# Two graph layers in fp32: layer-norm scale and shift folded into the next weights, pairwise masks, and one value bias moved behind the output weights

## The chip, the cores and the metric

One core of one Trainium2 chip runs the whole kernel. The metric is the device time of the program in microseconds; the kernel before takes 3042.13 us, the median of three runs between 3041.22 and 3043.72 us. All arithmetic is in fp32.

## The reference

The input is `x`, 64 graphs of 256 nodes with 256 features, and `adj`, a 0/1 matrix of 256 by 256 for each graph. Two layers follow each other.

```python
# layer 0
h = gat(gat(x, adj, W1, a1), adj, W2, a2)            # softmax over leaky_relu(e) where adj > 0
h = layernorm(x + h) * g_ln1 + b_ln1
x = layernorm(h + relu(h @ w_ff1 + b_ff1) @ w_ff2 + b_ff2) * g_ln2 + b_ln2
# layer 1: 8 heads of 32; r is the relation, the value of adj
attn = softmax((x @ Wq + bq) @ (x @ Wk + bk).T / sqrt(32))
out = sum over r of (attn * (adj == r)) @ (x @ Wv[r] + bv[r])
x = layernorm(x + out @ Wo + bo) * g1 + beta1
x = layernorm(x + gelu(x @ W1 + b1) @ W2 + b2) * g2 + beta2
```

Four layer norms end the four stages: after the two graph attentions, after the first feed-forward, after the relational attention, and after the second feed-forward. Since `adj` is 0 or 1, only two relations occur; the kernel uses `Wv[0]` for all weights and the difference `Wv[1] - Wv[0]` for the masked ones.

## The kernel before

The 64 graphs are worked in 32 pairs. `whole_way(pair)` takes one pair through everything: `gat_layers`, `feed_forward` with relu, `attention`, `feed_forward` with gelu. Each of these is a generator that yields before each group of matmuls and names what the group waits for. Up to four pairs are on their way at a time, so that TensorE has groups of several pairs to choose from.

The order of the work is planned while the program is built. `put(engine, us, emit, *events, rank=...)` hands a piece of work for an engine other than TensorE to a planner, with the time that the piece is expected to take and the events it waits for; `took(us)` does the same for a group of matmuls. `run` steps through this planned time, takes from each engine's pieces the ready one of lowest rank, and for TensorE prefers groups that have been ready for `SLACK` = 0.3 us. `keep_order` then fixes the instruction order of every engine as planned. Each engine works its queue in that order: an instruction that waits holds up all behind it. Buffers have planned release times too (`needs`, `frees`). So other expected times or other pieces change the order on every engine.

The parts that the change touches:

- `layernorm` (L572): DVE computes mean and variance of the rows in two halves (L582, L583) and two small operations, variance plus eps (L584) and the negated mean (L585). GpSimd raises to the power -0.5 (L588) and multiplies (L589); this short part on GpSimd is called the root below. ACT normalises the rows in place (L593). DVE multiplies by g and adds beta, two operations of 128x512 (L598). The rows so scaled are both the input of the next stage and its residual.
- `transposed` (L607): the rows are turned on DVE in 32x32 blocks (L618), stored to DRAM and gathered (L623, L629), which gives them transposed for the next matmuls. In five cases, named in `hurried`, TensorE transposes instead (`transposed_on_tensor`, L649 and L653). `add_rows` (L570) later adds the residual to a matmul's result.
- `feed_forward`: the first matmuls (L681) follow a scheme with seven products per block instead of eight, with copies by ACT (L687), additions by DVE (L392) and activations by ACT (L693); then the second matmuls (L712).
- `attention`: queries, keys (L754) and values (L759) by the same scheme; queries and keys get their bias from ACT (L769), both value blocks from DVE (L775). `scores` (L796) fills four PSUM banks, one for each of four heads; ACT takes the exponential of each (L803), DVE multiplies each by the mask (L807) and adds its halves (L811). `products` (L825, L828) uses these tiles, and DVE divides (L837, L838). `into_rows` (L847) multiplies by `Wo`.
- `relieve`, `relieve_values` and `reliefs` (from L904): once at the start. Since b2 of a stage is added to beta beforehand (L899), the residual carries it; the biases of the next stage are corrected for it by small matmuls (L912, L921), and sums of weight blocks are made (L340). The queries' weights are scaled (L936).

At the start SP issues the loads of all weights one after the other, and DVE has the additions of L899 and L901 in its queue among the first pairs' work.

Of the kernel before, what the change touches and what calls it, by code (L numbers as in the profile page):

```python
# [18 lines left out]
P = 128  # L19
# [6 lines left out]
EVEN = 1e-37  # L26
HURRIED = 2
# [5 lines left out]
def two_layers(ctx: ExitStack, tc: tile.TileContext, t: dict, out: bass.AP, flag: bass.AP):  # L33
# [77 lines left out]
    a2, w1T = (work.tile([P, 512], F32, name="a", bufs=2 * HQ) for _ in range(2))  # L111
    junk = work.tile([P, N], F32, name="h", bufs=2 * HQ)
    w1T = w1T.rearrange("p (c m) -> p c m", c=KC)
# [28 lines left out]
    free = {name: [0.0] * n for name, n in (("bank", 8), ("a", 2 * HQ), ("m", 2 * HQ), ("h", 2 * HQ), ("yb", 1), ("yT", 2), ("yTa", 1),  # L142
# [372 lines left out]
    def gat_layers(pair, to, loads):  # L515
# [36 lines left out]
        for b in range(2):  # L552
            yield [e[b][1], loads[2]], None, 1
            ps = bank()
            for i in range(2):
                for j in range(2):
                    nc.tensor.matmul(ps[:, i * D:(i + 1) * D], lhsT=e[b][0]["e"][:, j, i * P:(i + 1) * P],  # L557
                                     rhs=z[:, 2 * b + j, :D], start=j == 0, stop=j == 1)
            there = took(1.73)
            frees_at(there.time, ["e"])  # L560
            added = add_rows(to["x"], ps, b, there, loads[2])
            transposed(to["x"], layernorm(to["x"], ln[0], b, added, biased[0]), normal, b, pair, 0)
# [9 lines left out]
    def layernorm(r, gb, b, *events):  # L572
        g, beta, _ = gb
# [3 lines left out]
        def statistics():  # L577
            nonlocal st, mv, rstd, less
            st, mv = small.tile([P, 2, 6], F32, name="st"), small.tile([P, 2, 2], F32, name="mv")
            rstd, less = small.tile([P, 2], F32, name="rstd"), small.tile([P, 2], F32, name="less")  # L580
# [3 lines left out]
            nc.vector.tensor_scalar(rstd, mv[:, :, 1], EPS, None, ALU.add)  # L584
            nc.vector.tensor_scalar(less, mv[:, :, 0], -1.0, None, ALU.mult)  # L585

        def root():
            nc.gpsimd.tensor_tensor(rstd, rstd, mhalf[:, :2], ALU.pow)  # L588
# [6 lines left out]
        def scale():  # L595
            both = r[:, of_graph(b), :]
            for v, op in ((g, ALU.mult), (beta, ALU.add)):
                nc.vector.tensor_tensor(both, both, v.rearrange("p (k d) -> p k d", k=1).to_broadcast([P, 2, D]), op)  # L598

        there = put("vector", 1.22, statistics, *events)  # L600
        there = put("gpsimd", 1.2, root, there)
        return put("vector", 1.2, scale, put("scalar", 0.8, normalise, there))
# [5 lines left out]
    def transposed(y, ready, to, b, pair, stage):  # L608
# [23 lines left out]
        there = put("vector", 0.62, turn, ready, needs="yb")  # L632
        there = put("sync", 0.4, store, there, lag=1.3, kb=256, frees=["yb"])
        to[b] = put("sync", 1.75, gather, there, *([to[0]] if b else []), lag=1.7, kb=64, needs=None if b else "yT")

    def transposed_on_tensor(y, to):

        for b in range(2):
# [17 lines left out]
            to[b] = put("scalar", 0.55, copy, took(0.75), frees=["bank"])  # L656

    def feed_forward(y, normal, w, func, relieved, gb, pair, stage):
# [6 lines left out]
        if hurried(pair, stage):  # L665
            yield from transposed_on_tensor(y, normal)
# [38 lines left out]
        for b in range(2):  # L705
# [12 lines left out]
            normal[b] = layernorm(y, gb, b, add_rows(y, p2, b, there), *([biased[1]] if onwards else []))  # L718
            if onwards:
                transposed(y, normal[b], normal, b, pair, 1)  # L720
        done_with("ff")


    def attention(y, normal, pair, all_adj):


        if hurried(pair, 1):
            yield from transposed_on_tensor(y, normal)
# [13 lines left out]
        a, m, h = ([[None] * HQ for _ in range(4)] for _ in range(3))  # L742
# [29 lines left out]
        def with_bias_v(r, b, event, frees=()):  # L772
            def copy():
                bias = bv[:, r * D:(r + 1) * D].rearrange("p (k d) -> p k d", k=1).to_broadcast([P, 2, D])
# [13 lines left out]
        def scores(n):  # L788
# [10 lines left out]
            adj = all_adj[:, of_graph(b), :].rearrange("p k n -> p (k n)")  # L799

            def weight(o):
                a[n][o] = work.tile([P, 512], F32, name="a", bufs=2 * HQ)
                nc.scalar.activation(a[n][o], ps[o], AF.Exp)  # L803

            def mask(o):
                m[n][o] = work.tile([P, 512], F32, name="m", bufs=2 * HQ)
                nc.vector.tensor_tensor(m[n][o], a[n][o], adj, ALU.mult)  # L807

            def halves(o):
                h[n][o] = work.tile([P, N], F32, name="h", bufs=2 * HQ)  # L810
                nc.vector.tensor_tensor(h[n][o], a[n][o][:, :N], a[n][o][:, N:], ALU.add)  # L811

            there = [put("scalar", 0.48, lambda o=o: weight(o), there, rank=0, function="exp", needs="a", frees=["bank"])
                     for o in range(HQ)]
            masked.append([put("vector", 0.61, lambda o=o: mask(o), there[o], rank=0, needs="m") for o in range(HQ)] +
                          [put("vector", 0.34, lambda o=o: halves(o), there[o], rank=0, needs="h") for o in range(HQ)])

        def products(n):
            b, c = divmod(n, KC)
            po = bank()  # L820
            for r, e in enumerate((a[n], m[n])):
                for jc in range(2):
                    for o in range(HQ):
                        at = r * D + (c * HQ + o) * DH
                        nc.tensor.matmul(po[o * DH:(o + 1) * DH, :N], lhsT=v[:, b, jc, at:at + DH],  # L825
                                         rhs=e[o][:, jc * N:(jc + 1) * N], start=r == jc == 0, stop=r == jc == 1)
            for o in range(HQ):
                nc.tensor.matmul(po[o * DH:(o + 1) * DH, N:], lhsT=ones, rhs=h[n][o], start=True, stop=True)  # L828
            there = took(2.2)
            frees_at(there.time, ["a", "m"] * HQ + ["h"] * (HQ - 1))  # L830
            s, to = h[n][0], qk[:, 0, c, b * N:(b + 1) * N]
# [568 lines left out]
```

## Time and profile before

| | |
|---|---|
| median of the runs | 3042.13 us |
| span of the profiled execution | 3047.2 us (the page gives no other time for it) |
| TensorE matmuls, 19146 records | 2996.3 us busy |
| TensorE weight loads | 2452.5 us |
| VectorE (DVE), 5993 instructions | 2556.8 us |
| ScalarE (ACT), 4096 instructions | 1752.5 us, of it 70 table loads of 1.283 us |
| GpSimd (POOL), 518 instructions | 252.6 us |
| DMA | mean 68 GB/s, 20.6% of 16 engines on the main queue |

Every fp32 matmul instruction leaves two records. The busy time of an engine is the time in which at least one of its instructions is under way; matmuls overlap their neighbours, so a matmul of 128x256 lasts 0.38 us in the records although they start 0.216 us apart when TensorE runs full. The weight loads (PEld) run beside the matmuls. In a line of a group the columns are line, engine, operation, tiles, shapes and count, then the busy time, the mean of one in ns, the idle time of the engine just before, and what ended it. In a line of waits the columns are the engine and tile that waited, for whom, the total in us, how many times, and the longest.

### The profile page before, as it was taken

The numbers are of one execution on the slowest core, as the hardware profiler recorded it, in microseconds if no ns is written. First come the engines' busy times: TensorE is split into PE (matmuls) and PEld (weight loads), VectorE is DVE, ScalarE is ACT, GpSimd is POOL, SyncE is SP. The second block draws the span as 40 slices with busy tenths as digits, with TensorE's granted clock in tenths as the row PEclk, the third lists the DMA queues.
The fourth block names the chain that finished last, engine by engine and source line by source line (L and its number), as shares of the span: only waits on it lengthen the run. The fifth ranks groups of instructions, "written<-read, shape, count | busy, mean of one in ns | idle before, by whom it ended". The sixth has DMA issues, their size and how long they took to land.

```text
span 3047.2 us, 52870 instructions
## 1 busy us (share of the span) xinstructions
PE 2996.3 (98%) x19146; PEld 2452.5 (80%) x19146; DVE 2556.8 (84%) x5993; ACT 1752.5 (58%) x4096; POOL 252.6 (8%) x518
## 2 busy tenths in 40 slices
PE   7999999999999999999999999999999999999998
PEld 6887788878888888888888888888888888788876
DVE  5888988788988888888889888889888898888875
ACT  4556666556556556555565565565555655555654
POOL 0100010001100001100001000011000011000100
PEclk8999999999999999999999999999999999999999
DMA  5211041212212222112222112221122221122100
GB/s 186 74 47 61 32 127 54 70 56 84 70 40 66 77 84 77 53 53 70 84 84 77 39 60 77 84 77 62 50 68 79 84 77 52 52 71 70 49 1 22
DMA packets 211147, 205.76 MB, mean 68 GB/s; under 512 B 22336, under 2 KB 170432, under 8 KB 210880
## 3 DMA queue, kind: packets, MB, share of 16 engines
q1 hardware_dynamic: 210464, 202.06, 20.6%
q8 instruction: 153, 2.51, 0.4%
q14 instruction: 114, 0.93, 0.1%
q10 hardware_dynamic: 416, 0.26, 0.0%
HBM read 137.51 MB, written 64.73 MB: 66 GB/s over the span
## 4 chain that ended last, share of the span: by engine, by line
PE 63%; DVE 25%; DMA 6%; ACT 2%; SPq 1%; issue 1%; POOL 0%; DVEq 0%; ACTq 0%; POOLq 0%
PE ps L712 21%; PE ps L681 15%; PE ps L825 5%; DVE x L598 4%; PE ps L759 4%; PE ps L754 4%; PE ps L544 3%; DVE h L837 3%; PE ps L796 3%; DMA home<-yb 3%; DVE st L582 2%; DVE m L807 2%; PE ps L557 2%; DMA rows<-row 2%; DVE ff L392 2%; PE ps L847 2%
## 5 line engine op out<-in xcount | busy, mean ns | idle before, releaser
L712 PE MATMUL ps<-w_L_gnn_w_ff,ff 128*128 128x256 f32 x2048 | 470.9, 381 | 0.0
L712 PE MATMUL ps<-w_L_gnn_W,ff 128*128 128x256 f32 x2048 | 456.1, 380 | 1.8 <-ACT ff L693 1.8
L593 ACT ACTIVATE x<-x,less,rstd 128x256 f32<-128x256 f32 x512 | 279.2, 596 | 294.8 <-POOL less L589 294.7
L712 PEld LDWEIGHTS ps<-w_L_gnn_w_ff,ff 128*128 128x128 f32 x2048 | 386.6, 190 | 61.5 <-issue 9.8
L712 PEld LDWEIGHTS ps<-w_L_gnn_W,ff 128*128 128x128 f32 x2048 | 388.2, 190 | 57.6 <-ACT ff L693 2.6
L588 POOL TENSOR_TENSOR rstd<-rstd,mhalf 128x2 f32<-128x2 f32 x256 | 198.3, 775 | 2765.7 <-DVE less L585 2638.0
L807 DVE TENSOR_TENSOR m<-a,adj 128x512 f32<-128x512 f32 x512 | 350.1, 684 | 57.9 <-ACT a L803 57.8
L803 ACT ACTIVATE a<-ps 128x512 f32<-128x512 f32 x512 | 268.0, 604 | 222.6 <-PE ps L796 222.5
L681 PE MATMUL ps<-yT,w_L_gnn_W1p 128*128 128x256 f32 x1280 | 315.2, 382 | 4.7 <-ACT ff L687 2.4
L392 DVE TENSOR_TENSOR ff<-ps,ff 128x512 f32<-128x512 f32 x384 | 262.7, 685 | 66.4 <-PE ps L681 58.3
L681 PE MATMUL ps<-yT,w_L_gnn_w_ff1p 128*128 128x256 f32 x1280 | 308.8, 382 | 6.8 <-ACT ff L687 5.9
L681 PEld LDWEIGHTS ps<-yT,w_L_gnn_w_ff1p 128*128 128x128 f32 x1280 | 240.6, 190 | 50.8 <-ACT ff L687 18.8
L687 ACT ACTIVATE ff<-ps 128x512 f32<-128x512 f32 x384 | 223.9, 590 | 98.4 <-PE ps L681 97.6
L681 PEld LDWEIGHTS ps<-yT,w_L_gnn_W1p 128*128 128x128 f32 x1280 | 240.2, 190 | 48.2 <-ACT ps L835 8.5
L837 DVE RECIPROCAL h<-ps 128x256 f32<-128x256 f32 x128 | 223.4, 1746 | 21.3 <-PE ps L828 20.9
L509 ACT ACTIVATE xw<-xw,rs 128x258 f32<-128x258 f32 (+1 forms) x256 | 115.9, 502 | 200.7 <-DVE rs L504 200.6
L693 ACT ACTIVATE ff<-ff,c_L_gnn_b_ff 128x256 f32<-128x256 f32 x384 | 171.6, 504 | 97.4 <-DVE ff L392 97.0
L693 ACT ACTIVATE ff<-ff,c_L_gnn_b 128x256 f32<-128x256 f32 x384 | 173.3, 501 | 85.0 <-DVE ff L392 83.8
L811 DVE TENSOR_TENSOR h<-a 128x256 f32<-128x256 f32 x512 | 213.9, 418 | 0.0
L582 DVE BATCH_NORM_STATS2 st<-x 128x6 f32<-128x256 f32 x512 | 206.0, 402 | 0.9
L570 DVE TENSOR_TENSOR x<-ps,x 128x512 f32<-128x512 f32 x256 | 170.2, 682 | 16.4 <-PE ps L712 9.3
L769 ACT ACTIVATE qk<-ps,bqk 128x256 f32<-128x256 f32 x256 | 106.6, 468 | 112.2 <-PE ps L754 111.9
(128 smaller groups left out, 5008.1 us busy)
## 6 DMA issues: line engine op xcount, KB each, us to landing
home<-yb SPq DMA_DIRECT2D x182, 256.0 KB, 2.0
yT<-home SPq DMA_DIRECT2D x728, 64.0 KB, 2.0
rows<-row SPq DMA_DIRECT2D x60, 512.0 KB, 4.0
input<-in_xT SPq DMA_DIRECT2D x32, 512.0 KB, 5.1
x<-in_x SPq DMA_DIRECT2D x32, 512.0 KB, 3.8
out<-x SPq DMA_DIRECT2D x32, 512.0 KB, 5.1
input<-in_adjT SPq DMA_DIRECT2D x30, 512.0 KB, 4.5
v<-in_adjT SPq DMA_DIRECT2D x2, 512.0 KB, 7.3
```

The source lines that it names most:

```text
L392: nc.vector.tensor_tensor(self.target(c, h), self.bank[bank], self.target(c, h), ALU.add)
L582: nc.vector.bn_stats(st[:, j, :], rows[j])
L588: nc.gpsimd.tensor_tensor(rstd, rstd, mhalf[:, :2], ALU.pow)
L593: nc.scalar.activation(rows[j], rows[j], AF.Identity, bias=less[:, j:j + 1], scale=rstd[:, j:j + 1])
L681: nc.tensor.matmul(to, lhsT=w1[:, a, (t + slab) * P:(t + slab + 1) * P], rhs=b, **flags)
L687: return put("scalar", 0.5, lambda: nc.scalar.activation(target(c, h), blocks.bank["x"], AF.Copy), event, rank=-1)
L693: evacuated[h][m] = put("scalar", 0.4, lambda m=m, to=to, source=source: nc.scalar.activation(to, source, func, bias=b1[:, m:m + 1]), even ...
L712: nc.tensor.matmul(p2[:, j * D:(j + 1) * D], lhsT=f[m][:, (2 * j + b) * P:(2 * j + b + 1) * P], rhs=w2[:, m, :], start=m == 0, stop=m == N ...
L803: nc.scalar.activation(a[n][o], ps[o], AF.Exp)
L807: nc.vector.tensor_tensor(m[n][o], a[n][o], adj, ALU.mult)
L811: nc.vector.tensor_tensor(h[n][o], a[n][o][:, :N], a[n][o][:, N:], ALU.add)
L837: there = put("vector", 1.68, lambda: nc.vector.reciprocal(s, po[:, N:]), there, rank=0)
```

## The change

1. The rows that leave a layer norm toward the next matmuls are no longer scaled and shifted: they are turned as soon as ACT has normalised them. The factor g is multiplied into the next stage's first weights at the start (`with_g`), and beta, by small matmuls, into its biases (`with_beta`, `on_rows`). The residual is scaled and shifted on GpSimd, in place, after the turn has read the rows (`scaled`); `add_rows` waits for that. The last layer norm's rows, which are the output, are scaled on GpSimd too. The two small operations of the statistics go from DVE to GpSimd.
2. Exponentials of two heads share a tile of 128x1024; DVE makes masks and half sums for two heads with one instruction. The buffers hold the same bytes in half as many tiles.
3. The bias of the first value block is no longer added to the values: since the softmax weights of a row sum to one, it is multiplied by `Wo` at the start and added to the row that the residual gets. The values of that block are copied out of PSUM by ACT, without a bias.
4. SP loads three more small columns net, one more bias row and one more bias column, and in part in another order.

The planner's expected times change with the pieces: 0.9 for the statistics, 1.5 for the root, with rank 0, 1.2 for each GpSimd operation with rank 2, 1.14 and 0.61 for the masks and half sums of two heads.

```diff
-        transposed(to["x"], layernorm(to["x"], ln[0], b, added, biased[0]), normal, b, pair, 0)
+        transposed(to["x"], layernorm(to["x"], b, added), normal, b, pair, 0)
...
         def root():
+            nonlocal rstd, less
+            rstd, less = small.tile([P, 2], F32, name="rstd"), small.tile([P, 2], F32, name="less")
+            nc.gpsimd.tensor_scalar(less, mv[:, :, 0], -1.0, None, ALU.mult)
+            nc.gpsimd.tensor_scalar(rstd, mv[:, :, 1], EPS, None, ALU.add)
             nc.gpsimd.tensor_tensor(rstd, rstd, mhalf[:, :2], ALU.pow)
             nc.gpsimd.tensor_tensor(less, less, rstd, ALU.mult)
...
-        def scale():
+        there = put("vector", 0.9, statistics, *events)
+        there = put("gpsimd", 1.5, root, there, rank=0)
+        return put("scalar", 0.8, normalise, there)
+
+    def scaled(r, gb, b, *events):
+
+        def scale(v, op):
             both = r[:, of_graph(b), :]
-            for v, op in ((g, ALU.mult), (beta, ALU.add)):
-                nc.vector.tensor_tensor(both, both, v.rearrange("p (k d) -> p k d", k=1).to_broadcast([P, 2, D]), op)
-
-        there = put("vector", 1.22, statistics, *events)
-        there = put("gpsimd", 1.2, root, there)
-        return put("vector", 1.2, scale, put("scalar", 0.8, normalise, there))
+            nc.gpsimd.tensor_tensor(both, both, v.rearrange("p (k d) -> p k d", k=1).to_broadcast([P, 2, D]), op)
+
+        there = put("gpsimd", 1.2, lambda: scale(gb[0], ALU.mult), *events, rank=2)
+        return put("gpsimd", 1.2, lambda: scale(gb[1], ALU.add), there, gb[2], rank=2)
...
         there = put("vector", 0.62, turn, ready, needs="yb")
+        to["scaled", b] = scaled(y, ln[stage], b, there)
...
-            normal[b] = layernorm(y, gb, b, add_rows(y, p2, b, there), *([biased[1]] if onwards else []))
+            normal[b] = layernorm(y, b, add_rows(y, p2, b, there, normal["scaled", b]))
             if onwards:
                 transposed(y, normal[b], normal, b, pair, 1)
+            else:
+                normal[b] = scaled(y, ln[3], b, normal[b])
...
         def with_bias_v(r, b, event, frees=()):
+            if r == 0:
+                return put("scalar", 0.5, lambda: nc.scalar.activation(target_v(r, b), of_v.bank["x"], AF.Copy), event, rank=-1)
+
...
-            def mask(o):
-                m[n][o] = work.tile([P, 512], F32, name="m", bufs=2 * HQ)
-                nc.vector.tensor_tensor(m[n][o], a[n][o], adj, ALU.mult)
-
-            def halves(o):
-                h[n][o] = work.tile([P, N], F32, name="h", bufs=2 * HQ)
-                nc.vector.tensor_tensor(h[n][o], a[n][o][:, :N], a[n][o][:, N:], ALU.add)
...
+            def weight(q):
+                a[n][q] = work.tile([P, 2, 512], F32, name="a", bufs=HQ)
+                for k in range(2):
+                    nc.scalar.activation(a[n][q][:, k], ps[2 * q + k], AF.Exp)
+
+            def mask(q):
+                m[n][q] = work.tile([P, 2, 512], F32, name="m", bufs=HQ)
+                nc.vector.tensor_tensor(m[n][q], a[n][q], adj, ALU.mult)
+
+            def halves(q):
+                h[n][q] = work.tile([P, 2, N], F32, name="h", bufs=HQ)
+                nc.vector.tensor_tensor(h[n][q], a[n][q][:, :, :N], a[n][q][:, :, N:], ALU.add)
...
-    bv = on_all("L1_gnn_bv", 2 * D)
+    bv, bv0 = on_all("L1_gnn_bv1", D), column("L1_gnn_bv0")
+    less_bv = work.tile([P, 2, 512], F32, name="ff", bufs=NF // 2)[:, 0, :D]
+    nc.sync.dma_start(less_bv, bass.AP(tensor=t["L1_gnn_bv"].tensor, offset=t["L1_gnn_bv"].offset, ap=[[0, P], [1, D]]))
...
+    def with_g(blocks, g, there, more=1.0):
+
+        def scale():
+            for _, c, at in BLOCKS:
+                nc.vector.tensor_scalar(blocks(at), blocks(at), g[:, c:c + 1], more, ALU.mult, ALU.mult)
+
+        return put("vector", 1.4, scale, *there, rank=5)
...
+        g, beta = ln[1][3]
+        q, k = (slice(n * P, (n + 1) * P) for n in range(2))
+        there = [with_beta(bqk[:, n], block(wqk, rows), P, beta) for n, rows in enumerate((q, k))]
+        values = [on_rows(bv, beta, lambda c: block(wv)(1, c)), with_beta(bv0, block(wv), D, beta)]
+        scaled_bias = put("vector", 0.15, lambda: nc.vector.tensor_scalar(bqk[:, 0], bqk[:, 0], SCALE, None, ALU.mult), there[0])
+        there = [with_g(lambda at, rows=rows: wqk[:, at, rows], g, there[n:n + 1], (SCALE, 1.0)[n]) for n, rows in enumerate((q, k))]
+        put("vector", 0.0, lambda: None, block_sums(wqk, put("vector", 0.0, lambda: None, *there)), scaled_bias,
+            block_sums(wv, with_g(lambda at: wv[:, at], g, values)), event=relieved[1])
+        yield values, None, 1
+        on_rows(ln[1][1], bv0, lambda c: wo[:, c], projected, event=ln[1][2])
```

## The prediction

> **What bounds the kernel now.** I read the engine table first, then the stretches, then what TensorE (PE) waited for in the steady part, then the groups on the engines that the change touches.
>
> ```profile
> span 3047.2 us, 52870 instructions
> ...
> PE 2996.3 (98%) x19146; PEld 2452.5 (80%) x19146; DVE 2556.8 (84%) x5993; ACT 1752.5 (58%) x4096; POOL 252.6 (8%) x518
> ```
>
> PE is busy for all but 50.9 us of the span. VectorE (DVE) at 84% is next; GpSimd (POOL) is nearly free. The stretches (columns: length, then busy time and instructions of PE, PEld, DVE, ACT, POOL, then clock and DMA) tell where the 50.9 us lie:
>
> ```profile
> 0.00:30.00 30.00, 18.06 (x88) 15.45 (x89) 12.89 (x40) 9.51 (x21) 0.70 (x6) 0.89 0.80 252
> 30.00:62.00 32.00, 22.75 (x119) 19.75 (x118) 19.07 (x64) 12.71 (x34) 2.34 (x4) 0.79 0.58 180
> ...
> 100.00:2900.00 2800.00, 2786.37 (x17629) 2282.06 (x17631) 2397.14 (x5595) 1628.58 (x3807) 236.67 (x482) 1.00 0.21 67
> 2900.00:2980.00 80.00, 77.91 (x679) 59.92 (x672) 64.22 (x128) 47.83 (x111) 4.74 (x10) 1.00 0.01 1
> 2980.00:3012.00 32.00, 29.50 (x246) 22.80 (x244) 23.37 (x59) 15.46 (x34) 4.25 (x8) 1.00 0.05 17
> 3012.00:3036.00 24.00, 23.70 (x110) 20.49 (x110) 9.08 (x19) 10.56 (x23) 0.88 (x2) 1.00 0.07 23
> 3036.00:3047.00 11.00, 0.00 (x0) 0.00 (x0) 3.14 (x11) 1.09 (x2) 0.88 (x2) 0.63 0.18 54
> ```
>
> 21.2 us are lost in the first 62, only 13.6 in the 2800 us between 100 and 2900, 4.9 from there to 3036, and 11 behind the last matmul. What PE waited for in the middle:
>
> ```profile
> PE ps L681 <- ACT ff L687: 7.4, 15, 1.4
> PE ps L754 <- ACT qk L769: 1.3, 3, 0.8
> PE ps L544 <- ACT xw L509: 1.0, 1, 1.0
> PE ps L825 <- DVE m L807: 1.0, 3, 0.3
> ```
>
> It waits for ScalarE (ACT), hardly for DVE. So the kernel is bound by PE's own work, and DVE's 84% is cover, not path. The groups to be changed:
>
> ```profile
> L593 ACT ACTIVATE x<-x,less,rstd 128x256 f32<-128x256 f32 x512 | 279.2, 596 | 294.8 <-POOL less L589 294.7
> ...
> L588 POOL TENSOR_TENSOR rstd<-rstd,mhalf 128x2 f32<-128x2 f32 x256 | 198.3, 775 | 2765.7 <-DVE less L585 2638.0
> L807 DVE TENSOR_TENSOR m<-a,adj 128x512 f32<-128x512 f32 x512 | 350.1, 684 | 57.9 <-ACT a L803 57.8
> ```
>
> ACT already stands 294.7 us behind POOL's small root; ACT is what PE waits for. That is the thread to watch.
>
> [...]
>
> ```profile
> 51.38 0.70 POOL L588 TENSOR_TENSOR rstd<-rstd,mhalf 128x2 f32<-128x2 f32 x1 [50.07 <-DVE less L585]
> ...
> 57.46 1.20 POOL L588 TENSOR_TENSOR rstd<-rstd,mhalf 128x2 f32<-128x2 f32 x1 [5.06 <-DVE less L585]
> ```
>
> The second ran beside L598 on DVE (two SBUF inputs), the first beside an add from PSUM. That DVE is held by POOL no run here shows[...].
>
> **The change, part by part.** *DVE.* Gone are the 512 scale and shift operations of L598 (88.6+88.6+86.6+86.4 = 350.2 us) and the two small operations L584 and L585 (43.5+41.4 = 84.9). [...] Half of L775 goes to ACT: -43.9. In all -552.8. New at the start are 20 multiplications of weights by g against 4 of L936: between 0.22 us (a 128x128 at L936) and 0.69 (a 128x512 two-input), some 7 us. DVE ends near 2011 us, 66%. Of this PE gets nothing directly: its waits for DVE in the middle are the 1.0 us above and 0.6 for a yT. What it can get is a calmer ACT, since ACT waits for DVE before L693 and L509; the ceiling is the 13.6 us.
>
> *ACT.* 64 copies of values out of PSUM at the 590 ns of L687, which has that shape, are 37.8 us. In the compiled order ACT loads its tables 96 times instead of 70 in this part of the program; at the 1283 ns of the trace's loads, 33.4 us more. ACT ends near 1824 us, 60%; it has room, but each load stands ahead of whatever is queued behind it, 1.3 us at a time.
>
> *POOL.* [...] The roots get two small operations each, about the 209 ns of L589: 256 x 0.42 = 107. [...] The scaled rows are wanted only by the residual addition (L570 before) at the end of the next stage, some tens of us later, so the new wait there costs nothing in the steady part. What is queued behind a scale operation is the next root. [...] the two small operations add 0.4 and take 0.25 off DVE. On the other hand the two L598, 1.38 us, are off the way from a layer norm to its transposition. So the rows come about 1 us earlier, and the ACT instruction (L593) about 0.3 us later.
>
> *DVE held by POOL.* [...] With 34% of DVE free I take no cost for it on PE and keep 0 to 15 us for the range.
>
> *PE.* Four tiny matmuls more; the changes of kind (128 groups of scores, 128 of products) are the same number. Matmuls that wait for two semaphores or more rise from 329 to 443. In the trace of before 507 such extra waits stand in PE's queue, and 94 of them beside a start that is 0.1 us late: 114 x 94/507 x 0.1 = 2 us; 0 to 11.
>
> *Start.* SP issues three more DMAs ahead of the row that DVE's L899 waits for (beta before, b2 now): at 0.47 us each, 1.4 us. Behind that instruction on DVE stand the weights of the attention, behind them ACT's L509, and for that PE stood 9.3 us at L557. So +1.4 on the path; five DMAs in all stand ahead of the third pair's loads, which only ACT's copy of the adjacency meets (high end 3). The multiplications by g fall in DVE's 3.2 and 3.4 us waits before L446 and cost nothing there.
>
> *End.* [...] In the last pair's transpositions by PE, 1.4 us of L598 leave a way on which PE idled 2.5 us between 2980 and 3012: -1.5 (0 to -2.5).
>
> *Sum:* start +1.4, PE's waits +2, end -0.4, middle 0 (from -10 to +15): +3. The profiled execution took its span, 3047.2 us, for which the page gives no other time; that is 5.1 us above the median of the runs, 3042.1. I work the difference in the span and put it on the median: 3045.
>
> **Rivals.** *The middle fills.* With rows 1 us earlier and a freer DVE, ten of the 13.6 us vanish and the extra semaphores hide: 3042.1 + 1.4 - 0.4 - 10 = 3033. For it: 1.4 us less on every layer norm. Against: PE's waits end on ACT's L687, which the change doesn't shorten.
>
> *Late roots.* A root that is behind a scale piece keeps ACT at its L593; behind it stand L687 and L693, and behind these PE. This is the case on the other side: 256 roots, each costing PE 0.06 us on average, are 15 us: 3042.1 + 1 + 15 = 3058. It decides from about 0.02 us per root (6 us). For it: 294.7 us of ACT already wait there, 102 times in the middle with up to 9.2 us[...]. Against: PE has four pairs to choose from and lost only 13.6 us despite those waits.
>
> *Table loads.* A third of the 33.4 us on ACT reaching PE, with the 1 us of start and end: 3054.
>
> **How the numbers follow.** Forecast (PE full as before, 3036 to 3050) 0.40; the middle fills (3026 to 3037) 0.28; late roots (3047 to 3075) 0.26; table loads (3047 to 3062) 0.06. About 6 us, 0.2%, is what the runs can tell from no change. Faster: 0.26 from the second case and 0.02 from the first, 0.28. Slower: 0.25 and 0.06 from the last two and 0.07 from the first, 0.38. The rest, 0.34, is the same. The range 3028 to 3064 leaves out some 0.1 at each end.
>
> **What would show it.** Right: DVE near 2010 us, ACT near 1824 with 26 table loads more, [...]PE still 98%, idle 10 to 17 us between 100 and 2900, and 1 to 3 us more before the first L557. Late roots: ACT's wait for POOL above 400 us and PE's for L687 grown. Wrong: a POOL piece over 2 us, masks much over 1.3 us (DVE held by POOL), or PE's busy share below 97%.

## The result: 36 us slower, outside the range

The changed kernel takes 3078.78 us (3077.64 to 3079.83, four runs), the kernel before, in runs beside it, 3042.93 us (the ratio is 1.0117, 95% interval 1.0103 to 1.0132). 3045 had been forecast, with a range up to 3064. ACT's sum came much as forecast; DVE's sum and TensorE's idle time didn't. Top of the page of the changed kernel:

```profile
span 3075.9 us, 52423 instructions
...
PE 3010.9 (98%) x19154; PEld 2454.7 (80%) x19154; DVE 2234.0 (73%) x4411; ACT 1835.1 (60%) x4186; POOL 1032.2 (34%) x1542
```

DVE lost 323 us of work, ACT gained 83, POOL 780. PE still reads 98%: at that rounding the share can't show 28.7 us of a longer span. (The spans differ by 28.7 us and the medians by 36: other spans here are about 2 us under the time of their run, as 3075.9 is under 3077.64 in the changed kernel, so the 3047.2 of the trace before stands for a run of some 3049, 7 above the median, and losses read from that trace may be too high by so much in all.) The stretches can (columns as before):

```profile
0.00:30.00 30.00, 20.84 (x87) 17.78 (x88) 13.00 (x42) 9.45 (x21) 0.69 (x6) 0.89 0.80 249
30.00:62.00 32.00, 20.81 (x126) 17.49 (x125) 18.73 (x62) 12.53 (x35) 5.20 (x9) 0.79 0.67 183
100.00:2900.00 2800.00, 2768.66 (x17463) 2257.53 (x17462) 2073.75 (x4063) 1697.26 (x3863) 963.09 (x1438) 1.00 0.21 67
```

The first 62 us lose 20.4 us (21.2 before). The middle loses 31.3 us against 13.6: the place is the steady part. What PE waited for there:

```profile
PE ps L689 <- ACT ff L695: 22.9, 29, 1.7
PE ps L545 <- ACT xw L510: 2.6, 1, 2.6
PE ps L689 <- ACT ps L850: 1.8, 1, 1.8
```

L689 and L695 are the old L681 and L687: the first product of the feed-forwards, and ACT's copies that it needs; 7.4 us have become 22.9. Busy time hides the small stalls, since a matmul's record overlaps the next: at the first product a record lasts 379 ns, and the starts lie 216 ns apart (medians). If I sum, over the whole trace, the distance of each matmul's start from the start before it, by line, the first product takes 829.9 us where it took 802.5: 27.4 of the span's 28.7 us. Counted above the 216 ns of a full PE, 17.4 of these 27.4 lie in starts over 330 ns after the one before, and 10.1 in starts 230 to 330 ns after. All other lines together are within 2 us of before. The groups on the page of the changed kernel:

```profile
L594 ACT ACTIVATE x<-x,less,rstd 128x256 f32<-128x256 f32 x512 | 279.3, 594 | 418.8 <-POOL less L590 414.9
...
L822 DVE TENSOR_TENSOR m<-a,adj 128x1024 f32<-128x1024 f32 x256 | 325.4, 1271 | 20.6 <-ACT a L818 20.5
...
L604 POOL TENSOR_TENSOR x<-x,b_L_gnn_g_ln 128x512 f32<-128x512 f32 x128 | 168.7, 1318 | 274.5 <-DVE yb L623 138.3
...
L589 POOL TENSOR_TENSOR rstd<-rstd,mhalf 128x2 f32<-128x2 f32 x256 | 189.1, 739 | 21.3
```

ACT waits 414.9 us for roots (294.7 before), and from the end of the statistics to the end of the root it takes 1.95 us on average (1.49 before). A mask's mean is 1271 ns, longer than the 1217 of the same kernel with GpSimd's pieces made short (below). The timeline of the changed kernel shows why (start, length, engine, line, and in brackets the idle time before it and its releaser):

```profile
738.15 0.69 DVE L826 TENSOR_TENSOR h<-a 128x512 f32<-128x512 f32 x1
738.29 1.67 POOL L604 TENSOR_TENSOR x<-x,b_L_gnn_g 128x512 f32<-128x512 f32 x1 [1.20 <-ACT x L594]
738.75 2.30 DVE L822 TENSOR_TENSOR m<-a,adj 128x1024 f32<-128x1024 f32 x1
740.04 2.13 POOL L604 TENSOR_TENSOR x<-x,b_L_gnn_beta 128x512 f32<-128x512 f32 x1
740.97 1.75 DVE L826 TENSOR_TENSOR h<-a 128x512 f32<-128x512 f32 x1
```

Where these instructions of the two engines meet, both grow: the mask takes 2.30 us for 1.21, the half sum behind it 1.75 for 0.68, each while a POOL piece is under way, and POOL's pieces 1.67 and 2.13 for 1.27 (the median of all 512). Elsewhere in the same timeline a late root ends on PE:

```profile
2063.81 1.09 ACT L594 ACTIVATE x<-x,less,rstd 128x256 f32<-128x256 f32 x2 [0.80 <-POOL less L590]
...
2064.81 0.57 ACT L695 ACTIVATE ff<-ps 128x512 f32<-128x512 f32 x1
...
2065.29 0.89 ACT L701 ACTIVATE ff<-ff,c_L_gnn_b_ff 128x256 f32<-128x256 f32 x2
...
2066.09 1.08 ACT L594 ACTIVATE x<-x,less,rstd 128x256 f32<-128x256 f32 x2
...
2067.07 0.89 ACT L701 ACTIVATE ff<-ff,c_L_gnn_b_ff 128x256 f32<-128x256 f32 x2
2067.86 1.06 ACT L695 ACTIVATE ff<-ps 128x512 f32<-128x512 f32 x2
...
2068.49 1.13 PE L689 MATMUL ps<-yT,w_L_gnn_w_ff1p 128*128 128x256 f32 x4 [1.33 <-ACT ff L695]
```

ACT works without a pause behind the 0.80 us of waiting, and the copy of 2067.86 that PE needs is last in its queue: PE's matmuls had ended by 2067.16 in the records, and the copy started 0.70 us later, behind an L701 that started at 2067.47.

### The profile page after: what moved, and what is told of

The parts are those of the page before. It is cut to its first block, busy times and chain, and to the rows that moved or that the text cites. A ratio compares the mean times of both kernels' runs of the same rounds, so it can differ in the third digit from the quotient of the medians.

```text
span 3075.9 us, 52423 instructions
## 1 busy us (share of the span) xinstructions
PE 3010.9 (98%) x19154; PEld 2454.7 (80%) x19154; DVE 2234.0 (73%) x4411; ACT 1835.1 (60%) x4186; POOL 1032.2 (34%) x1542
## 4 chain that ended last, share of the span: by engine, by line
PE 79%; DVE 10%; ACT 3%; DMA 3%; POOL 2%; issue 2%; SPq 1%; DVEq 0%; POOLq 0%; ACTq 0%
PE ps L720 24%; PE ps L689 20%; PE ps L840 6%; PE ps L764 6%; PE ps L769 6%; PE ps L809 4%; PE ps L545 3%; PE ps L529 3%; PE ps L862 2%; PE ps L843 2%; DVE e L502 2%; DVE x L571 2%; DVE st L581 1%; PE ps L558 1%; DMA home<-yb 1%
## 5 line engine op out<-in xcount | busy, mean ns | idle before, releaser
L587 POOL TENSOR_SCALAR less<-mv 128x2 f32<-128x2 f32 x256 | 65.4, 255 | 1596.6 <-DVE mv L582 1561.4
L594 ACT ACTIVATE x<-x,less,rstd 128x256 f32<-128x256 f32 x512 | 279.3, 594 | 418.8 <-POOL less L590 414.9
L720 PEld LDWEIGHTS ps<-w_L_gnn_w_ff,ff 128*128 128x128 f32 x2048 | 387.9, 190 | 57.2 <-issue 4.3
L393 DVE TENSOR_TENSOR ff<-ps,ff 128x512 f32<-128x512 f32 x384 | 261.1, 683 | 163.6 <-PE ps L689 127.1
L822 DVE TENSOR_TENSOR m<-a,adj 128x1024 f32<-128x1024 f32 x256 | 325.4, 1271 | 20.6 <-ACT a L818 20.5
L689 PE MATMUL ps<-yT,w_L_gnn_W1p 128*128 128x256 f32 x1280 | 316.1, 384 | 10.9 <-ACT ff L695 7.4
L689 PE MATMUL ps<-yT,w_L_gnn_w_ff1p 128*128 128x256 f32 x1280 | 312.4, 384 | 12.3 <-ACT ff L695 12.3
L689 PEld LDWEIGHTS ps<-yT,w_L_gnn_W1p 128*128 128x128 f32 x1280 | 238.3, 190 | 61.8 <-ACT ff L695 17.9
L689 PEld LDWEIGHTS ps<-yT,w_L_gnn_w_ff1p 128*128 128x128 f32 x1280 | 241.3, 191 | 56.6 <-ACT ff L695 16.7
L695 ACT ACTIVATE ff<-ps 128x512 f32<-128x512 f32 x384 | 221.1, 589 | 92.0 <-PE ps L689 90.1
L604 POOL TENSOR_TENSOR x<-x,b_L_gnn_g_ln 128x512 f32<-128x512 f32 x128 | 168.7, 1318 | 274.5 <-DVE yb L623 138.3
L701 ACT ACTIVATE ff<-ff,c_L_gnn_b_ff 128x256 f32<-128x256 f32 x384 | 174.4, 509 | 49.4 <-DVE ff L393 48.8
L604 POOL TENSOR_TENSOR x<-x,b_L_gnn_g 128x512 f32<-128x512 f32 x128 | 166.1, 1298 | 94.4 <-ACT x L594 74.8
L589 POOL TENSOR_TENSOR rstd<-rstd,mhalf 128x2 f32<-128x2 f32 x256 | 189.1, 739 | 21.3
L701 ACT ACTIVATE ff<-ff,c_L_gnn_b 128x256 f32<-128x256 f32 x384 | 172.0, 502 | 31.6 <-DVE ff L393 31.0
```

Of the source, the lines that this page charges most:

```text
L393: nc.vector.tensor_tensor(self.target(c, h), self.bank[bank], self.target(c, h), ALU.add)
L594: nc.scalar.activation(rows[j], rows[j], AF.Identity, bias=less[:, j:j + 1], scale=rstd[:, j:j + 1])
L604: nc.gpsimd.tensor_tensor(both, both, v.rearrange("p (k d) -> p k d", k=1).to_broadcast([P, 2, D]), op)
L689: nc.tensor.matmul(to, lhsT=w1[:, a, (t + slab) * P:(t + slab + 1) * P], rhs=b, **flags)
L695: return put("scalar", 0.5, lambda: nc.scalar.activation(target(c, h), blocks.bank["x"], AF.Copy), event, rank=-1)
L701: evacuated[h][m] = put("scalar", 0.4, lambda m=m, to=to, source=source: nc.scalar.activation(to, source, func, bias=b1[:, m:m + 1]), even ...
```

## The experiments

There are three theories. *Late roots*: ACT waits for a GpSimd that has scale and shift to do. *Held VectorE*: GpSimd's reading of SBUF stretches DVE's instructions, and what waits for DVE comes late. *Order*: the planner, given other pieces, puts another order on every engine (planned: 38% of the first product's matmuls in unbroken runs of 24 and more, 6% before), and that order is worse. Each expectation stands as it was written before its run; times are medians of the runs, the other columns of the table come from one trace each. "PE idle" below is 2800 minus PE's busy time between 100 and 2900 us, "first product" the sum of its starts' distances as above.

| kernel | us | PE idle | first product |
|---|---|---|---|
| before / changed | 3042.4 / 3078.8 | 13.6 / 31.3 | 802.5 / 829.9 |
| masks_only | 3039.8 | 10.0 | 798.5 |
| values_only | 3050.8 | 15.6 | 805.1 |
| fold_only | 3070.5 | 23.6 | 823.2 |
| short_gpsimd | 3053.5 | 14.9 | 812.3 |
| busy_gpsimd | 3064.7 | 21.0 | 818.4 |
| scale_on_vector | 3072.4 | 33.3 | 825.3 |
| scale_vector_values_vector | 3053.8 | 14.6 | 805.8 |
| masks_slack / masks_slack_04 | 3068.3 / 3048.8 | 26.5 / 15.5 | 821.9 / 802.6 |
| after_slack_04 | 3088.7 | 34.3 | 843.5 |
| masks_root_later | 3052.7 | 14.0 | 803.5 |
| masks_root_planned_later | 3058.8 | 24.6 | 815.7 |
| after_root_planned_later | 3087.5 | 37.6 | 814.1 |
| after_roots_on_vector | 3090.8 | 36.4 | 839.4 |
| fold_vector_roots_on_vector | 3074.4 | 33.1 | 822.4 |
| after_fixed_norm | 3067.5 | 23.2 | 818.4 |
| masks_fixed_norm | 3042.2 | 12.9 | 798.1 |
| short_fixed_norm | 3048.6 | 13.9 | 809.6 |

("before" is the median over its runs beside the last three, which the sums at the end use.) Set against the span of the same trace, the first product is where most of the time went in most rows; two exceptions, masks_root_later and after_root_planned_later, are told below.

**One part at a time.** Part 2 alone on the kernel before (masks and half sums for two heads at a time):

```diff
-                nc.vector.tensor_tensor(m[n][o], a[n][o], adj, ALU.mult)
+                nc.vector.tensor_tensor(m[n][q], a[n][q], adj, ALU.mult)
```

> The kernel before with part 2 of the change alone: exponentials, masks and half sums of two heads in one tile. Theory 'order' (the fold changes the planned order so that a whole first feed-forward runs without another pair's matmuls in between, and each copy by ACT is then waited for): no such runs arise here (104 of 1792 products of L681 in runs of 24 or more, as before), so 3035 to 3047 us. Rival 'coarse pieces' (two exponentials and a double mask hold up ACT and DVE): 3055 or more.

3039.80 us, a ratio of 0.9989 (0.9982 to 0.9996): the fastest of all kernels here, and the version that beats both. The first value block alone, copied by ACT:

```diff
+            if r == 0:
+                return put("scalar", 0.5, lambda: nc.scalar.activation(target_v(r, b), of_v.bank["x"], AF.Copy), event, rank=-1)
```

> The kernel before with the first value block copied by ACT without its bias (a bias of zeros is left out). Order: 178 of 1792 products in runs of 24 or more, close to before, so 3040 to 3050 us. Rival 'ACT load' (38 us more on ACT, with 6 table loads more, make the copies late): 3055 or more.

3050.83 us, 1.0028 (1.0019 to 1.0037): 8 us lost, with six table loads more on ACT. The fold alone (the changed kernel with parts 2 and 3 taken back):

> The changed kernel with parts 2 and 3 undone: fold into the weights, scale and shift on GpSimd alone (both value blocks get the bias row of the second on DVE, zeros here). Order: 598 of 1792 products in runs of 24 or more, 686 in the changed kernel, 104 before; so most of the loss is here, 3065 to 3080 us. Rivals 'coarse pieces' and 'ACT load': 3035 to 3050.

3070.49 us, 1.0092 (1.0075 to 1.0108). The three add to 28 + 8 - 3 = 33 of the 36 us: most of the loss comes in with the fold, its new order included.

**Is it GpSimd or the order?** The changed kernel with its order kept on every engine, and its scale and shift on GpSimd working on 1 of the 256 columns, which leaves the other 255 unscaled (one of two changed lines):

```diff
-            both = r[:, of_graph(b), :]
+            both = r[:, of_graph(b), :1]
```

> The changed kernel with the same order of instructions on every engine, but the 512 scale and shift operations on GpSimd touch one column of each row block instead of 256 (g is one and beta zero, the rest stays unscaled). They shrink from 1.3 to about 0.2 us, and with them both the hold on DVE and the wait of a root behind them. Theory 'order': 3065 to 3080 us, as the order stays. Rival 'GpSimd' (late roots and DVE held[...]): 3040 to 3055.

3053.50 us: 25.3 of the 36 us are back with the order unchanged, so the order alone falls as the explanation. PE's wait for the copies in the middle, and then DVE's mask:

```profile
PE ps L689 <- ACT ff L695: 13.0, 25, 1.1
```

```profile
L822 DVE TENSOR_TENSOR m<-a,adj 128x1024 f32<-128x1024 f32 x256 | 311.4, 1217 | 20.8 <-ACT a L818 20.5
```

22.9 us became 13.0 (waits between 100 and 2900 us); the mask (a group on DVE) is at 1217 ns again, and DVE's busy time at 2143.6: the hold had been 90 us of DVE. Next, GpSimd occupied but not reading:

```diff
+            for _ in range(3):
+                nc.gpsimd.memset(filler, 0.0)
```

> The changed kernel in the same order on every engine; each of its 512 scale or shift instructions on GpSimd works on 1 of the 256 columns (so 255 columns stay unscaled, which is nothing in numbers where g is 1 and beta 0), and three GpSimd memsets of 128x400 on a tile that nothing reads follow it, so that GpSimd is occupied for about as long as by the full instruction (1.1 to 1.3 us), but reads nothing from SBUF in that time. The run with short instructions (3053.5 us) freed GpSimd and left VectorE unheld at once; this one takes only the reading of SBUF away. Theory 'late roots' (ACT waits for a GpSimd that is busy with a scale or a shift, and its copies for TensorE come late): 3073 to 3081 us, ACT's wait for POOL at L594 at or over 415 us, TensorE's wait for ACT's copies at 28 to 36 us. Theory 'held VectorE' (instructions of VectorE with both inputs in SBUF are stretched while GpSimd works on SBUF, and VectorE's results come late): 3050 to 3058 us, VectorE's busy time near 2145 us as with short instructions, TensorE's wait for ACT's copies at 14 to 18 us, though ACT waits for POOL as long as in the changed kernel. If the memsets stretch VectorE too (busy time near 2230), the run tells nothing of the two apart.

3064.66 us, halfway: neither theory's number. The memsets don't hold DVE's instructions with two inputs in SBUF, as its group of masks shows; PE's wait in the middle lies between 22.9 and 13.0 too:

```profile
L824 DVE TENSOR_TENSOR m<-a,adj 128x1024 f32<-128x1024 f32 x256 | 311.4, 1216 | 21.3 <-ACT a L820 20.8
```

```profile
PE ps L691 <- ACT ff L697: 17.9, 27, 1.2
```

So 14 us go with the reading of SBUF, and 11 with an occupied GpSimd (at most: the replacement takes 1.52 us where the piece took 1.31, and roots ended 2.01 us after the statistics, not 1.95). Both theories hold a part of the truth.

**How much is an order worth?** One planner number, the same instructions:

```diff
-SLACK = 0.3
+SLACK = 0.5
```

> The kernel with paired masks (3039.8 us) with one number of the planner changed (SLACK 0.3 to 0.5), so that the same instructions come in another order: 55% of the first products of the feed-forward in unbroken runs of 16 and more against 37%, 245 runs against 249, four more loads of ACT's table. What it differs from 3039.8 is what a mere change of the order is worth here: theory 'order' expects +3 to +10 us; if the order matters little, within 3 us.

3068.33 us, 28.5 more than with 0.3, nearly three times the upper end of what I expected. PE's wait in the middle rises to 17.0 us (3.9 with 0.3), without any scale or shift on GpSimd:

```profile
PE ps L681 <- ACT ff L687: 17.0, 25, 1.9
```

Two more draws with 0.4:

> The kernel with paired masks, SLACK 0.3 to 0.4: the same instructions in one more order (37% of the first products in runs of 16 and more and 268 runs; the order of 3039.8 us had 37% and 249, that of 3068 had 55% and 245). If the long stays in one strand make an order bad, this one is near 3040 us (3037 to 3048); if any redrawn order loses, since the durations fit the one that was kept, 3050 to 3070.

> The changed kernel, SLACK 0.3 to 0.4: the same instructions in another order (31% in runs of 24 and more against 38%, six table loads fewer). If the order is a draw with a scatter of 10 to 20 us around a mean that the change has raised: 3060 to 3095 us, not below 3055. A time under 3050 would say that the change itself costs nothing and that its order was merely a bad draw.

3048.79 and 3088.69 us. For the paired masks three orders give 3040, 3049, 3068; for the changed kernel two give 3079 and 3089. The change stands above its counterpart at either number (by 39 and 40 us), but a draw moves the time as much as most parts of the change do.

**Scale and shift on VectorE.**

```diff
-            nc.gpsimd.tensor_tensor(both, both, v.rearrange("p (k d) -> p k d", k=1).to_broadcast([P, 2, D]), op)
+            nc.vector.tensor_tensor(both, both, v.rearrange("p (k d) -> p k d", k=1).to_broadcast([P, 2, D]), op)
...
-        there = put("gpsimd", 1.2, lambda: scale(gb[0], ALU.mult), *events, rank=2)
+        there = put("vector", 0.6, lambda: scale(gb[0], ALU.mult), *events, rank=2)
```

> The changed kernel with the 512 instructions of scale and shift on VectorE at the same rank 2 (cost for the planner 0.6 us), the roots alone on GpSimd; the planner orders anew. VectorE gets 512 x 0.68 = 348 us and loses the hold of some 90 us: about 2490 us, 82%. Both theories of a busy GpSimd ('late roots' and 'held VectorE') expect most of the 25 us back that short instructions gave: 3050 to 3058 us, if VectorE at 82% is not late itself. A rival, 'crowded VectorE', says that VectorE needs the room: 3065 to 3085 us, with TensorE waiting for VectorE at L393 and L846.

> As the run before, and the first value block is copied by VectorE again (with a row of zeros in the place of the bias), so that only the fold (without GpSimd) and the masks are left of the change. Moving that block to ACT alone cost 8.5 us on the kernel before. If the parts add up, this lies 6 to 11 us below the run before, near 3045 us, and the fold by itself, without GpSimd, costs nothing beside the masks' 3039.8: 3040 to 3048. If the fold's longer unbroken runs of the first product of the feed-forward (31% of these matmuls in runs of 24 and more against 6%) cost by themselves, 3048 to 3056 us.

3072.38 and 3053.78 us. The first gave back little, where both theories of a busy GpSimd had expected 3050 to 3058; the number lies in the range of the rival, a crowded VectorE, but PE's wait for DVE (6.4 us) is at another line (L360) than it said. Here, too, the planner drew a new order, so the run doesn't tell crowding from order. Taking the values back from ACT is worth 18.6 us here against 8 in the old order: the parts don't add once the order is drawn again.

**The root's own price.** In the order of the paired masks, two instructions more in each root, whose result nothing uses:

```diff
+            for _ in range(2):
+                nc.gpsimd.tensor_scalar(dummy, rstd, EPS, None, ALU.add)
```

> The kernel with paired masks (3039.8 us), in its own order on every engine, with two more GpSimd instructions on 128x2 (some 0.23 us each, on a tile that nothing reads) in every root, so that each root ends about 0.5 us later, as the roots of the changed kernel do (end of statistics to end of root 1.95 us against 1.45). Theory 'late roots by themselves': the changed kernel's extra lateness cost it 11 us or more in its order, so it costs as much here: 3048 to 3056 us. Theory 'what stands ahead of the copies' (a late root costs TensorE only where the normalisation that waits for it stands in ACT's queue ahead of a copy that TensorE waits for; in this kernel 8 such normalisations stand ahead of late copies, in the changed kernel 51): at most 4 us, 3038 to 3044.

3052.72 us (3046.82 to 3055.43), 13 more, with roots 2.13 us after the statistics for 1.45: my "at most 4" fell. PE idle grew by 4.0 of these 13 and the first product by 5; the rest is spread over small stalls. So the changed kernel's four instructions in place of two ought to cost too, and taking two back to DVE to pay (one of the two lines):

```diff
-            nc.gpsimd.tensor_scalar(less, mv[:, :, 0], -1.0, None, ALU.mult)
+            nc.vector.tensor_scalar(less, mv[:, :, 0], -1.0, None, ALU.mult)
```

> The changed kernel in its own order and with its own planner numbers, with the two short instructions of the root (256 times -mean and variance+eps, 0.25 and 0.24 us on GpSimd) back on VectorE, where they took 0.17 and 0.16 us: the median root ends some 0.27 us sooner after its statistics (1.39 us against 1.66), and 124 us of GpSimd are gone; VectorE has 85 us more. With roots 0.68 us later the kernel with paired masks lost 13 us, that is 19 ns of the whole time for each ns; theory 'late roots by themselves' expects 5 to 9 us back: 3070 to 3074 us. Theory 'the order decides': within 3 us of 3078.8.

> The fold with scale and shift on VectorE, values on VectorE, paired masks (3053.8 us), in the same order, with the same two instructions back on VectorE. Nothing of the change is then left on GpSimd. Theory 'late roots by themselves': 5 to 8 us back, 3046 to 3049 us, and the other 6 to 9 us to the paired masks alone (3039.8) are the new order. Theory 'the order decides': 3051 to 3057 us.

3090.76 and 3074.42 us: 12 and 21 us worse, though roots now end 1.52 us after the statistics and ACT's wait for them fell from 415 to 364 us. What grew is DVE (2234 to 2304 us), and PE's wait at the first product (here L688) for DVE's additions, from 0.7 to 8.6 us; the waits of after_roots_on_vector:

```profile
PE ps L688 <- ACT ff L694: 19.6, 29, 1.2
PE ps L688 <- DVE ff L393: 8.6, 13, 1.7
```

So earlier roots alone are no gain when DVE pays for them. 60 to 70 us more of DVE, less than the hold's 90, do damage of 12 to 21 us: the same order of size.

**Moving the wait by plan.** The root's result planned 1.5 us later:

```diff
-        there = put("gpsimd", 1.5, root, there, rank=0)
+        there = put("gpsimd", 1.5, root, there, rank=0, lag=1.7)
```

> The changed kernel with one number of the planner changed: the root's result is planned 1.5 us later (lag 0.2 to 1.7), so that the planner puts ACT's normalisation later in ACT's queue, behind copies that are ready sooner; no instruction is added or taken away, the order changes. ACT's wait for POOL at L594 was 415 us in the changed kernel. Theory 'what stands ahead of the copies': that wait falls under 200 us, the normalisations ahead of late copies from 51 to under 25, and the time from 3078.8 to 3050 to 3068 us. Theory 'any order is as good as another here' (a long stay of TensorE in one strand is what costs): 3070 to 3085 us, as 32% of these matmuls are still in runs of 24 and more.

> The kernel with paired masks and the same one number: the root's result is planned 1.5 us later. ACT's wait for POOL at the normalisation should fall by half or more, from some 320 us. Theory 'what stands ahead of the copies': few normalisations stand there already (8), so little is to be had: 3034 to 3042 us. Theory 'any change of the order re-rolls the stalls': 3045 to 3070 us, as the change of SLACK gave 3068.

3087.51 and 3058.81 us. ACT's wait for roots fell to 251 and 271 us, and both kernels became slower. In after_root_planned_later, whose waits follow, stalls left the first product (814.1) and turned up at L545:

```profile
PE ps L545 <- ACT xw L510: 12.5, 8, 2.3
PE ps L689 <- ACT ff L695: 11.1, 22, 1.1
```

The theory "what stands ahead of the copies" isn't settled. If I count the normalisations that start in the 4 us before a copy that PE waited for, there are 60 in the changed kernel, 8 in the paired masks and 56 in after_root_planned_later: the later plan hardly changed what it was meant to change. And masks_slack, where PE waits 17.0 us for copies, has only 6: the theory doesn't describe that stall.

**The three terms apart.** Fixed numbers in the place of each row's own let ACT normalise without the root; the rows are then not truly normalised, and order and work stay but for two small fills at the start.

```diff
-                nc.scalar.activation(rows[j], rows[j], AF.Identity, bias=less[:, j:j + 1], scale=rstd[:, j:j + 1])
+                nc.scalar.activation(rows[j], rows[j], AF.Identity, bias=fixed[:, 0:1], scale=fixed[:, 1:2])
```

> The changed kernel in its own order; ACT's normalisation takes fixed numbers (bias 0, scale 0.9) in the place of each row's own, so that it doesn't wait for the root, which GpSimd still computes (the output is then only roughly normalised). The scales and shifts on GpSimd stay, and hold VectorE as before. Theory 'late roots' (through ACT's queue): ACT's 415 us of waiting for POOL vanish, TensorE's wait for ACT's copies falls from 23.5 to under 12 us, and the time to 3045 to 3060 us. Theory 'late VectorE': ACT then stands for VectorE instead; 3064 to 3075 us. Theory 'order alone': 3070 to 3080.

> The kernel with paired masks (3039.8 us) in its own order, the normalisation with the same fixed numbers. ACT's 332 us of waiting for POOL vanish. The old order has little to lose by them: theory 'order' and theory 'late VectorE': within 5 us, 3034 to 3041. Theory 'late roots by themselves' (roots 0.68 us later cost 13 us, so none at all give back as much): 3020 to 3033 us.

> The changed kernel in its own order with both: the short scale and shift on GpSimd (1 of 256 columns, 3053.5 us by itself) and the normalisation with fixed numbers, so that neither a late root nor a held VectorE is left. If the order by itself is what keeps the short version above the paired masks, this stays 8 to 16 us above masks_fixed_norm, at 3040 to 3052 us; if late roots explain all of it, it lies within 4 us of masks_fixed_norm.

3067.49, 3042.16 and 3048.63 us. With the fixed numbers PE's wait for the copies in the middle shrinks by less than a third, from 22.9 to 16.3 us. ACT waits for DVE instead (565 us in all for 300); PE's wait and ACT's in after_fixed_norm (L597 is the normalisation):

```profile
PE ps L692 <- ACT ff L698: 16.3, 21, 1.2
```

```profile
ACT x L597 <- DVE st L584: 180.9, 77, 7.1
ACT h L853 <- DVE qk L856: 176.2, 80, 5.3
```

| changed kernel's order | ACT waits for roots | ACT does not |
|---|---|---|
| full scale and shift on GpSimd | 3078.8 | 3067.5 |
| short ones | 3053.5 | 3048.6 |

The 36.4 us to 3042.4 divide so: GpSimd's long pieces without any wait for a root, 3067.5 - 3048.6 = 18.9; the waits for roots without long pieces, 3053.5 - 3048.6 = 4.9; what both cost only together, 6.4; what remains with neither, 3048.6 - 3042.4 = 6.2: the order with the values' copies on ACT, and all else that changed. Each rests on medians with some 2 us of scatter. The 18.9 may hold, beside the stretched DVE, a part for additions that wait for scaled rows, and for other work of a long GpSimd; busy_gpsimd, where GpSimd stays occupied and only the reading goes (and scaled rows, of one column, are ready sooner), put that at 14. In the old order the roots' waits are worth nothing (3042.2 against 3039.8), although making the roots later cost 13. That an order fitted to its durations loses when something comes late, and wins nothing when it comes early, would explain both; it isn't shown.

## Why the prediction was wrong

- *DVE held by POOL: no cost taken.* This step failed, and is the largest term. The hold was 90 us, with DVE at 73%, and by these runs it cost 14 to 19 us of the 36. "34% of DVE free" was no cover: free time on an average doesn't help an instruction whose result is waited for. By which wait the hold reaches PE isn't traced to the end: with short pieces PE's wait for ACT's copies falls from 22.9 to 13.0 us, but the sum of ACT's own waits for DVE is no sign (300 us in the changed kernel, 267 with short pieces, 449 before). The step's own range, 0 to 15, nearly held the cost; 0 was the wrong choice. Length alone doesn't tell what holds DVE: the root's power, 0.71 us in the changed kernel, is longer than a half sum of two heads (0.687), and held neither masks nor half sums (last section).
- *Late roots.* The mechanism of the rival was right in part: ACT's wait rose to 414.9 us ("above 400"), PE's for the copies grew. The root was put 0.3 us later for ACT, the two small operations at 0.4 (0.255 and 0.235 on average in the trace) and queueing, my estimate, which no trace showed, at 0.2; measured against the end of the statistics it is 0.46 later. The price, 15 us, was 4.9 alone and 11.3 together with the hold. The rival, put at 3058, lacked the hold and the order.
- *Middle 0.* The order, which I had counted only by its number of changes of kind and its tables, was no term of the sum. With the values' copies and the rest it is 6.2 us here, and single draws showed 9 to 28. That is the second failure: the range left out that any new set of pieces redraws the order.
- *The middle fills.* Nothing of it shows: with neither late roots nor holds (short_fixed_norm) PE idles 13.9 us, no less than before, though in another order.
- *Start +1.4.* The first L558 waits 10.6 us for ACT where it waited 9.3, but masks_only, with no DMA added, has 7.8, and the first 62 us as a whole lost 0.8 us less. Not settled at that size.
- *PE's further waits +2.* Starts 230 to 330 ns after the one before, outside the first product, cost 57.2 us before and 55.1 after: no sign of it.
- *End -0.4.* From the last matmul's start to the end of the span 11.6 us became 12.7: +1.1, as much as my estimate behind the -0.4 had put for GpSimd's two pieces and the root. In the 56 us up to the last matmul PE idled 2.8 us before (2980 to 3036) and 0.2 now (3007 to 3063): the gain came, some 2.6 for 1.5. The waits of 0.69 and 0.71 us around the last transposition, 1.4 in all, are among what went.
- *Sizes on the engines.* ACT 1835 for 1824, with 96 tables; POOL 1032, its piece 1.30 to 1.32 us; the mask of two heads without a hold 1.217 and the half sum 0.683 (short_gpsimd). What I had put for pieces, masks and half sums was an estimate that no trace showed. DVE 2234 for 2011: 90 are the hold; the rest is mostly a mistake in my sum. Instructions that follow each other on DVE overlap by 83 ns (median) in the records, and busy time counts that once. A removed one frees so much less than its mean: 1582 fewer instructions times 0.083 are 131 us, an estimate.
- *Signs.* "PE below 97%" couldn't show anything: 28.7 us are 0.9% of the span, and matmuls of 379 ns in the records, 216 ns from start to start, cover small gaps. Idle time in the stretch, 31.3 for "10 to 17", did. The sign of late roots came (414.9 us), and of the signs of a held DVE the longest POOL piece (2.25 us) and the longest mask (2.30); their means, 1.31 and 1.27, stayed under the marks.

## What to carry to other kernels

Where an engine with in-order instructions (here ACT, whose copy of 2067.86 stood for 0.70 us behind other work) feeds the one that bounds the kernel, judge a change by how much later its results come, not by the free share of the engine that gets slower. Ask, too, whether a partner that reads the same memory makes it slower, as GpSimd's pieces did here with DVE's masks (1271 ns on average for 1217). If a planner writes the order, first change one of its numbers with the work unchanged: that scatter (here 9 to 28 us) is the yardstick for any edit. Take a change apart: the part that was worth having here was the paired masks, 3 us.

## What the runs showed of the hardware

In the changed kernel GpSimd's pieces of 128x512 and DVE's masks of 128x1024 stretched each other: the 230 masks that overlapped no piece took 1.18 to 1.23 us, the other 26 up to 2.30 (median 1.69), and a piece up to 2.25 for 1.27. Compared with the run with short pieces, DVE's instructions with both inputs in SBUF were stretched (masks 1271 ns on average for 1217, half sums 723 for 683, L502 538 for 485), and so were multiplications and the like of one tile by a number or a column: on 128x512 weights (L947) 1036 ns on average for 479, on 128x4 351 for 170. Instructions with an input in PSUM (L393, 683 ns against 684) and the turning in blocks (702 against 702) were not. GpSimd's memsets of 128x400 (431 ns) left the masks at 1216 ns, but the four multiplications of weights took 742 beside them. The root's power on 128x2 is not like the large pieces: in the changed kernel eight masks and half sums of two heads started while one was under way, and took 1216 and 687 ns, no more than elsewhere. The power itself was stretched: in the kernel before, the 53 that started while an L598 alone was under way on DVE took 1.064 to 1.068 us, those beside an L392 (an input in PSUM) 0.69; the 1.20 of the prediction met an L598 and an L914.
